# Attention and mixture of experts on one core: pairs of heads whole instead of by halves, and the place of some loads

## The chip, the core and the metric

The kernel runs on one core of one Trainium2 chip. The metric is the device time of one execution in microseconds (us). The profile is one further execution of the same program, taken by the hardware profiler.

## The reference

One layer on x of shape (4, 1024, 256), in float32. First attention with 16 heads of width 16, whose queries and keys are turned by position, and a layer norm over the residual sum:

```
q, k, v = x @ wq.T, x @ wk.T, x @ wv.T           # 16 heads of 16
q_embed = softplus(q) * (cos, sin)(position)     # width 32
k_embed = softplus(k) * (cos, sin)(position + bias of the head)
attn = softmax(q_embed @ k_embed.T / 4)          # 1024 x 1024 for each head and batch
x = layernorm(x + (attn @ v) @ wo.T)
```

Then a mixture of 8 experts, of which each token takes two and which holds 640 rows at most, with a second layer norm:

```
gates = softmax(x @ router_w + router_b); the two best experts of a token; a place in each expert's list
h = gelu(rows of the expert @ w1 + b1); out = h @ w2 + b2
x = layernorm(x + sum over a token's experts of gate * out)
```

## The kernel before

The changed parts all lie in the attention. Two heads make a *pair*; a batch has 8 pairs (two groups f of four), so there are 32 pairs in all. All work on a pair is cut into 8 *steps*, and the main loop runs over 256 steps, n = 0 to 255, with 64 to a batch. The order of instructions on every engine is the order in which this loop emits them.

For each pair the kernel needs two things. First the row maxima: `score_half` makes a 128 x 512 block of scores (a matmul, L755, into one of three PSUM banks of the pool `ps_3`) and VectorE takes the largest of each row (L759). A pair has 32 such blocks. From them `max_parts` makes the negated maxima in two parts (VectorE L771, ScalarE casts L772 and L773, VectorE L777), and `max_rows` turns them with four transposes (L783) and copies the result to `mt` (ScalarE, L785). Second, the pass itself: `key_scores` makes the scores again with the keys on the partitions (L795), `exponentials` adds the maxima with a two-row matmul (L809) and takes the exponential on ScalarE (L816), and `weighted_values` multiplies with the values (16 matmuls, L836) one step later.

A *unit* is what shares one set of maxima and one accumulator: a whole pair over 8 steps, or half of the queries of a pair over 4 steps. Before the change the first four pairs go by halves (eight units), all others whole. The maxima of a unit must be ready before it starts, so its score blocks are spread over earlier steps by a planner: the list `due` says that all blocks of unit w must be given out by two steps before its start, `may` says that a pair's blocks may not begin earlier than one step before the start of the pair before it, and each step takes the smallest number of blocks that keeps all due times. In a step TensorE runs: two score blocks, the key scores of the first tile, a third block, the key scores of the second tile, a fourth block, L809, the weighted values of the step before (L836), then any further blocks, then what the list `todo` has for this step (projections, embeddings of later pairs, values). If the step before used a PSUM bank for other work, the third block moves behind the second tile.

When a unit ends, `collect` sends the sums from its accumulator to two places with six transfers (L869, L872). When a group of four pairs ends, `over_sums` loads the collected denominators (`den`, L882), takes the reciprocal on VectorE (L884), stores it (`over`, L886) and loads it spread over the partitions with eight transfers (`r`, L889). For the second group of a batch this happens in the first steps of the next one: the load of `den` is emitted at the end of step 64b+1, the reciprocal, the store and the eight loads at the end of step 64b+2, and the products with `r` at the ends of steps 64b+5 and 64b+6.

`load_qk(i)` loads queries and keys of pair i, 2 MB in 12 transfers: six for the first head of the pair (its half 0), then six for the second head. The tiles have three buffers. Pair n/8 + 2 is loaded at the top of each step n that is a multiple of 8; the loop starts with pair 1's load already emitted, and pair 2 is loaded at step 4. All these transfers are issued by the one queue of SyncE (SP), strictly in the order of emission; an issue that waits holds up those behind it.

Ahead of the loop a prologue makes the tables, the embeddings of the first pairs and the maxima of the first unit. In its last part come, in this order: the second block of values (`vals[1]`), the second half of the query rows (`mq1`: for each of two heads four matmuls L460 and a copy L468), `max_parts(0)`, `max_rows(0)`, the stores of the second half of the query embeddings (`q1`), the tables' stores, and the copies `once` that free the buffer which pair 1's load then takes.

Of the kernel before, what the change touches and what calls it, by code (L numbers as in the profile page):

```python
# [28 lines left out]
def kernel(  # L29
# [20 lines left out]
    E, _, HID = w1.shape  # L50
    HD = 16
    NT = S // P
    NF = 2
    FH = 8
    NU = NF * FH // 2
# [46 lines left out]
    with ExitStack() as actx:  # L102
# [106 lines left out]
        def bias_angles():  # L209
            ps = bank("pbp", True)[:, 0:NF]  # L210
            for g in range(2):
                nc.tensor.matmul(
                    ps, place[:, g].rearrange("p d a j -> p (d a j)"), bias_in[:, g::2],
                    start=(g == 0), stop=(g == 1),
                )
            nc.vector.tensor_scalar(pb, ps, -2.0 * math.pi, 0.0, ALU.max, ALU.min)
            nc.scalar.activation(s1, pb, AF.Sin, scale=0.25)
            nc.scalar.activation(c1, pb, AF.Sin, bias=half_pi, scale=0.25)
            nc.scalar.preload_act_table_set("natural_log_exp_and_others")

            nc.vector.scalar_tensor_tensor(s2, s1, 2.0, c1, ALU.mult, ALU.mult)
            nc.vector.tensor_tensor(c2, s1, s1, ALU.mult)
            nc.vector.tensor_scalar(c2, c2, -2.0, 1.0, ALU.mult, ALU.add)
            nc.vector.scalar_tensor_tensor(sb4, s2, 8.0, c2, ALU.mult, ALU.mult)
            nc.vector.tensor_scalar(nb4, sb4, -1.0, None, ALU.mult)
            nc.vector.tensor_tensor(cb4, s2, s2, ALU.mult)
            nc.vector.tensor_scalar(cb4, cb4, -8.0, 4.0, ALU.mult, ALU.add)
# [502 lines left out]
        nms, mts, avs, pts = {}, {}, {}, {}  # L730


        units = []
        starts, lasting = [], []
        for i in range(B * NU):
            for h in range(2) if i < NU // NF else (None,):
                starts.append(starts[-1] + lasting[-1] if units else 0)
                units.append((i, *divmod(i // (NU // NF), NF), i % (NU // NF), h))
                lasting.append(NT if h is None else NT // 2)
# [21 lines left out]
        def max_parts(w):  # L761


            nm = nms.pop(w)
            m = m_sb[w % 2].rearrange("p i (s c) -> p i s c", c=32)
            both = small.tile([P, 4, 4, 2], F32, tag="nm_parts", name=f"nm_parts_{w}")
            least, of = both[:, :, :, 0], nm
            if units[w][4] is not None:
                least = least.rearrange("p i (t h) -> p i t h", t=2)
                of = nm[:, :, 0:2, :].unsqueeze(2).to_broadcast([P, 4, 2, 2, 2])  # L770
            nc.vector.tensor_reduce(least, of, AX.X, ALU.min)  # L771
            nc.scalar.copy(m.bitcast(F32R)[:, :, :, 0], both[:, :, :, 0])  # L772
            nc.scalar.activation(  # L773
                both.bitcast(F32R)[:, :, :, 1], both[:, :, :, 0], AF.Copy, scale=-1.0
            )
            yield
            nc.vector.tensor_reduce(m[:, :, :, 1], both, AX.X, ALU.add)  # L777
# [73 lines left out]
        def by_rows(w):  # L851
            return units[w][1] < B - 1 or units[w][2] == 0
# [75 lines left out]
        def run(pieces):  # L928
            next(pieces, None)
# [21 lines left out]
        for b in range(B):  # L951
# [17 lines left out]
            for n in range(4):  # L969
                w, h = "qk"[n // 2], n % 2  # L970
# [32 lines left out]
        with tc.manual_schedule():  # L1003
            bias_angles()
            once("k", 0)
            for i in range(2):
                transpose_x(0, i, rotate=True)
            nc.scalar.dma_start(wv_sb, wv)
            for w in "kq":
                load_twice(w, 1, nc.scalar)  # L1010
            for _ in key_table(0):
                pass
            once("q", 0)

            made = {}

            def first(w, h):
                return embedding(
                    0, 0, w, h, fast=(w, h) != ("q", 1), tab=cs if w == "q" else kt0,
                    pauses=(KC - 1,), rotate=True, apart=h == 1, made=made,  # L1020
                )

            def moving(w, h):
                return move_first(w, halves[h], made[w, h])

            k0, q0, k1, q1 = first("k", 0), first("q", 0), first("k", 1), first("q", 1)
            for work in (k0, k0):
                run(work)
            for i in range(2, 4):
                transpose_x(0, i, rotate=True)  # L1030
            table = key_table(1)
            for work in (q0, table, table, q0, k0, table, k1, q0, table, k1):
                run(work)
            mk0, mq0 = moving("k", 0), moving("q", 0)
            for work in (mk0, mq0, mk0, mq0, q1):
                run(work)

            for i in range(2):
                score_half(0, 2 * i, 0, True)
            for work in (k1, q1, q1):  # L1040
                run(work)
            for i in range(2, 4):
                score_half(0, 2 * i, 0, True)
            for work in (mk0, mq0, mk0, mq0, k0, q0):
                run(work)
            mk1 = moving("k", 1)
            run(mk1)
            for i in range(4):
                score_half(0, 2 * i + 1, 0, True)
            for work in (mk1, mk1, mk1, k1):  # L1050
                run(work)
            vals = [values_in_two(0, 0, h, rotate=True) for h in range(2)]
            for h in range(2):
                for i in range(4):
                    score_half(0, 2 * i + h, 1, True)
                    if (h, i) in ((0, 3), (1, 1)):
                        run(vals[0])
            for _ in vals[1]:
                pass
            mq1 = moving("q", 1)  # L1060
            for _ in range(4):
                run(mq1)
            for _ in max_parts(0):
                pass
            max_rows(0, rotate=True)
            run(q1)
            for h in range(2):
                store_table(0, h, cs[:, :, halves[h]])
                store_table(1, h, kt0[:, :, halves[h]])
            once("k", 1)  # L1070
            once("q", 1)
            load_qk(1)
            late_constants()
# [10 lines left out]
        with tc.manual_schedule():  # L1084
            for n in range(NS):
                w, c = step_of[n]
                b, p, t = n // (NU * NT), n // NT % NU, n % NT
                if n % NT == 0 and n > 0 or n == NT // 2:
                    i = n // NT + 2
                    if i < B * NU:  # L1090
                        load_qk(i)
                    elif i - B * NU < 2:
                        experts[i - B * NU] = expert_weights(i - B * NU)


                third_last, others[0] = others[0], False
                items = [(score_half, *x) for x in ahead[n]]
                first, third, fourth, rest = items[:2], items[2:3], items[3:4], items[4:]
                if third_last:
                    third, fourth = [], third + fourth  # L1100
                for f, *args in first:
                    f(*args)
                if parts:
                    run(parts)
                    parts = None
                tiles = [key_scores(w, c, 0)]
                for f, *args in third:
                    f(*args)
                tiles.append(key_scores(w, c, 1))
                for f, *args in fourth:  # L1110
                    f(*args)
                exponentials(w, c, tiles)
                if n > 0:
                    weighted_values(*step_of[n - 1])
                for f, *args in rest:
                    f(*args)
                if n + 2 in starts:
                    parts = max_parts(starts.index(n + 2))
                    run(parts)
                if n + 1 in starts:  # L1120
                    max_rows(starts.index(n + 1))
                if c == 1 and w > 0 and not by_rows(w - 1):
                    normalize(w - 1)
                for f, args in todo.get(n, ()):
                    f(*args)
                if b > 0 and (p, t) in FINISH:
                    if b not in finishing:
                        finishing[b] = finish_batch(b - 1)
                    next(finishing[b], None)
            weighted_values(*step_of[NS - 1])  # L1130


        with tc.manual_schedule():
            b, n = B - 1, NT // 2
# [328 lines left out]
```

## Time and profile before

| what | us |
|---|---|
| median of 3 runs (1423.34 to 1423.67) | 1423.62 |
| the profiled execution, its own time | 1425.13 |
| its span from the first to the last instruction | 1423.3 |
| TensorE busy | 1365.4 |
| VectorE busy | 885.8 |
| ScalarE busy | 740.8 |
| granted TensorE clock, mean over the span | 0.983 |

Times in the profile count from the first instruction of the span. PE is TensorE (PEld its weight loads), DVE VectorE, ACT ScalarE, POOL GpSimd, SP SyncE; a small q behind the name is an engine's sequencer, which issues transfers. A row of the timeline gives start, duration, engine, line, operation, result<-operands, shape and count; in square brackets the idle time before it and what ended that. A matmul's end is modelled, and matmuls overlap, so the length of a step is best read from the start of one L809 row to the start of the next.

### The profile page before, as it was taken

To read this page: it belongs to the slowest core of one execution; us is meant where nothing else is said; L and a number is where in the kernel's file an instruction comes from. 1 tells how busy PE (TensorE), PEld (TensorE's weight loads), DVE (VectorE), ACT (ScalarE), POOL (GpSimd) and SP (SyncE) were. 2 spreads that over 40 slices of the span, in tenths; PEclk is the share of its full clock that TensorE was granted. 3 is DMA by queue.
4 is the path that set the end of the run, shared out by engine and by line. 5 is a ranking of instruction groups with operands and counts; after the bars stand their busy time and mean duration, and the time that the engine had idled before them with its cause. 6 is when DMAs were issued, how large, how long until landed. Compare 5 with 4: busy or idle time off the path is not lost. (4 is left out here: it accounts for less than half of the span.)

```text
span 1423.3 us, 24542 instructions
## 1 busy us (share of the span) xinstructions
PE 1365.4 (96%) x9362; PEld 863.9 (61%) x9362; DVE 885.8 (62%) x1931; ACT 740.8 (52%) x1025; POOL 408.3 (29%) x427
## 2 busy tenths in 40 slices
PE   7999999999999999999999999999996399999998
PEld 4655555655655565565556556655643277777776
DVE  7667666667876666777856577887734433333335
ACT  5665676565566656556575665656463122222221
POOL 5261043340002646100065530000310314444443
PEclk9999999999999999999999999999998599999999
DMA  6776476374543746454466462225210436334211
GB/s 192 214 206 194 141 200 189 86 228 113 138 123 96 229 143 182 112 165 97 139 184 193 106 186 70 64 74 128 75 66 1 141 114 207 111 117 135 84 44 56
DMA packets 107765, 190.20 MB, mean 134 GB/s; under 512 B 19553, under 2 KB 56642, under 8 KB 107520
## 3 DMA queue, kind: packets, MB, share of 16 engines
q1 hardware_dynamic: 97792, 169.90, 41.2%
q0 software_dynamic: 8736, 16.87, 3.9%
q10 hardware_dynamic: 1120, 1.87, 0.4%
q8 instruction: 74, 1.21, 0.4%
q14 instruction: 43, 0.35, 0.1%
HBM read 118.27 MB, written 73.63 MB: 135 GB/s over the span
## 5 line engine op out<-in xcount | busy, mean ns | idle before, releaser
L759 DVE TENSOR_REDUCE nm<-s 128x1 f32<-128x512 f32 x1024 | 646.9, 683 | 234.1 <-PE s L755 226.0
L816 ACT ACTIVATE pt<-st 128x1024 f32<-128x1024 f32 x512 | 496.1, 1021 | 364.1 <-PE st L809 363.6
L755 PE MATMUL s<-qk 128*128 128x512 f32 x1024 | 383.4, 434 | 3.6 <-DVE nm L759 2.2
L795 PE MATMUL st<-qk 128*128 128x512 f32 x1024 | 303.8, 398 | 2.6 <-ACT pt L816 2.6
L836 PE MATMUL av<-pt,va 128*32 128x256 f32 x4096 | 274.7, 385 | 0.5 <-ACT pt L816 0.5
L755 PEld LDWEIGHTS s<-qk 128*128 128x128 f32 x1024 | 177.9, 188 | 110.5 <-DVE nm L759 49.4
L795 PEld LDWEIGHTS st<-qk 128*128 128x128 f32 x1024 | 182.7, 188 | 63.5 <-ACT pt L816 29.2
L836 PEld LDWEIGHTS av<-pt,va 128*32 128x32 f32 x4096 | 107.1, 109 | 107.0 <-issue 61.6
L692 POOL DMA_INDIRECT slots_in<-held,scatter_idx x64 | 63.0, 984 | 290.9 <-DVE scatter_idx L688 213.6
L414 POOL TENSOR_TENSOR soft_q<-y_q,soft_q 128x512 f32<-128x512 f32 x15 | 19.3, 1285 | 439.7 <-ACT soft_q L410 439.7
L1364 PE MATMUL op<-w,h 128*128 128x256 f32 x640 | 144.1, 379 | 0.0
L1345 PE MATMUL hp<-slots_t,w 128*128 128x320 f32 x512 | 141.0, 437 | 0.0
L1364 PEld LDWEIGHTS op<-w,h 128*128 128x128 f32 x640 | 119.5, 190 | 15.9
L809 PE MATMUL st<-mt,ones_r 2*128 2x512 f32 x1024 | 128.8, 492 | 0.0
L1345 PEld LDWEIGHTS hp<-slots_t,w 128*128 128x128 f32 x512 | 98.4, 192 | 40.4 <-issue 1.0
L809 PEld LDWEIGHTS st<-mt,ones_r 2*128 2x128 f32 x1024 | 49.0, 182 | 88.5 <-issue 88.1
L1352 ACT ACTIVATE h<-hp,b_sb 128x640 f32<-128x640 f32 x64 | 50.8, 793 | 87.7 <-PE hp L1345 87.7
L1379 DVE TENSOR_TENSOR o<-op,b_sb 128x256 f32<-128x256 f32 x35 | 14.9, 424 | 94.7 <-PE op L1364 94.6
L1380 ACT ACTIVATE o<-o,w 128x256 f32<-128x256 f32 x35 | 17.8, 508 | 103.2 <-issue 72.3
L1382 POOL DMA_INDIRECT y_rank<-o,rows x35 | 35.9, 1024 | 101.2 <-ACT slots_t L1195 46.1
L1303 POOL DMA_INDIRECT out_dram<-row,rows x40 | 40.9, 1022 | 42.7 <-DMA out_dram<-row,rows 13.1
L420 POOL TENSOR_TENSOR e_k<-soft_k,tab_k 128x512 f32<-128x512 f32 x28 | 35.4, 1286 | 47.5 <-DMA tab_k<-table 47.1
(217 smaller groups left out, 1034.5 us busy)
## 6 DMA issues: line engine op xcount, KB each, us to landing
qk<-embed_q SPq DMA_DIRECT2D x248, 128.0 KB
qk<-embed_k SPq DMA_DIRECT2D x124, 256.0 KB
embed_k<-parts_k SPq DMA_DIRECT2D x64, 256.0 KB
embed_q<-parts_q SPq DMA_DIRECT2D x64, 256.0 KB
w<-in_w_dram SPq DMA_DIRECT2D x16, 1024.0 KB
y_rank<-zero SPq DMA_DIRECT2D x8, 1024.0 KB
tab_q<-table SPq DMA_DIRECT2D x14, 512.0 KB
tab_k<-table SPq DMA_DIRECT2D x14, 512.0 KB
```

What stands on the lines that cost most here:

```text
L692: nc.gpsimd.indirect_dma_start(out=scatter_views[2 * t + k], out_offset=bass.IndirectOffsetOnAxis(ap=scatter_idx[:, k, t : t + 1], axis=0) ...
L755: nc.tensor.matmul(ps, qk[:, 2 * h, lo : lo + P], qk[:, 2 * h + 1, j * HS : (j + 1) * HS], start=True, stop=True,)
L759: nc.vector.tensor_reduce(nms[w][:, i, s, j : j + 1], ps, AX.X, ALU.max, negate=True)
L795: nc.tensor.matmul(ps[:, x, :], qk[:, 2 * h + 1, k * P : (k + 1) * P], qk[:, 2 * h, q * HS : (q + 1) * HS], start=True, stop=False,)
L809: nc.tensor.matmul(tiles[t][:, x, :], ones_r[rows, :], mts[w][rows, :], start=False, stop=True,)
L816: nc.scalar.activation(pt, tiles[t], AF.Exp)
L836: nc.tensor.matmul(av[32 * s : 32 * (s + 1), to], va[f][:, k, 2 * p + h, :], e, start=(c == 0 and n == 0), stop=(last and n == 1),)
L1303: nc.gpsimd.indirect_dma_start(out=out_views[t], out_offset=bass.IndirectOffsetOnAxis(ap=to[:, 0, t : t + 1], axis=0), in_=row[:, t, :], i ...
L1345: nc.tensor.matmul(ps[:, i, 0:half], w1_sb[:, k, c * P : (c + 1) * P], s_t[:, k, i * half : (i + 1) * half], start=(k == 0), stop=(k == KC ...
L1352: nc.scalar.activation(h_t[:, c, :].rearrange("p (i n) -> p i n", i=2), ps[:, :, 0:half], AF.Gelu, bias=b1_sb[:, e, c : c + 1],)
L1364: nc.tensor.matmul(ps, h_t[:, c, t * P : (t + 1) * P], w2_sb[:, c, :], start=(c == 0), stop=(c == HC - 1),)
L1382: nc.gpsimd.indirect_dma_start(out=y_views[e * ST + t], out_offset=bass.IndirectOffsetOnAxis(ap=to[:, 1, t : t + 1], axis=0), in_=o_sb, in ...
```

## The change

Three things are changed. Only pair 0 goes by halves of its queries; pairs 1, 2 and 3 become whole units. In the prologue `max_parts(0)` moves ahead of the second block of values, and `max_rows(0)` moves between the first and the second matmul group of `mq1`, so that on ScalarE the two casts of the maxima come before the copies of values and query rows. In the loop the loads of steps 64, 128 and 192 (pairs 10, 18 and 26) move to the top of steps 67, 131 and 195, behind the transfers of `over_sums`.

```diff
+        BY_HALF = (0,)
         units = []
         starts, lasting = [], []
         for i in range(B * NU):
-            for h in range(2) if i < NU // NF else (None,):
+            for h in range(2) if i in BY_HALF else (None,):
...
+            for _ in max_parts(0):
+                pass
             for _ in vals[1]:
                 pass
             mq1 = moving("q", 1)
-            for _ in range(4):
-                run(mq1)
-            for _ in max_parts(0):
-                pass
+            run(mq1)
             max_rows(0, rotate=True)
-            run(q1)
+            for work in (mq1, mq1, mq1, q1):
+                run(work)
...
-                if n % NT == 0 and n > 0 or n == NT // 2:
+
+                if t == 0 and p > 0 or t == 3 and p == 0 and b > 0 or n == NT // 2:
                     i = n // NT + 2
                     if i < B * NU:
                         load_qk(i)
```

Here NT is 8, NU is 8, b is the batch, p the pair within the batch and t the step within the pair.

## The prediction

> **What bounds the kernel now.** I read the page first, then the list of waits, then the timeline round the moved loads and in the first steps, and last the transfers by windows.
>
> ```profile
> span 1423.3 us, 24542 instructions
> PE 1365.4 (96%) x9362; PEld 863.9 (61%) x9362; DVE 885.8 (62%) x1931; ACT 740.8 (52%) x1025; POOL 408.3 (29%) x427
> ...
> PEclk9999999999999999999999999999998599999999
> ...
> L759 DVE TENSOR_REDUCE nm<-s 128x1 f32<-128x512 f32 x1024 | 646.9, 683 | 234.1 <-PE s L755 226.0
> ...
> L755 PE MATMUL s<-qk 128*128 128x512 f32 x1024 | 383.4, 434 | 3.6 <-DVE nm L759 2.2
> ```
>
> TensorE is busy in nearly every slice of the loop, VectorE waits for it (226 us) and hardly the other way round. So in the loop only two things cost time: work on TensorE, and waits of TensorE. The length of a step, from L809 row to L809 row, shows both:
>
> ```profile
> 67.65 0.50 PE L809 MATMUL st<-mt,ones_r 2*128 2x512 f32 x4
> ...
> 71.49 0.50 PE L809 MATMUL st<-mt,ones_r 2*128 2x512 f32 x4
> ...
> 331.53 0.50 PE L809 MATMUL st<-mt,ones_r 2*128 2x512 f32 x4
> ...
> 335.01 0.50 PE L809 MATMUL st<-mt,ones_r 2*128 2x512 f32 x4
> ```
>
> Step 5 with five score blocks takes 3.84, step 68 with four takes 3.48. Two steps stand out later, 66 with 4.46 and 130 with 4.68, and the timeline and the waits say why:
>
> ```profile
> 326.46 0.55 DVE L884 RECIPROCAL den<-den 128x64 f32<-128x64 f32 x1 [1.93 <-DMA den<-sums]
> ...
> 327.61 0.51 PE L755 MATMUL s<-qk 128*128 128x512 f32 x1 [0.69 <-DVE nm L759]
> ```
>
> ```profile
> DVE den L884 <- DMA den<-sums: 5.0, 3, 2.1
> ```
>
> VectorE stands before the reciprocal of the denominators, the score blocks behind it keep their banks, TensorE waits. What makes `den` late is on SP's queue (start, time to issue):
>
> ```profile
> 311.52 2.98 SPq L485 DMA_DIRECT2D qk<-embed_q  x4
> ...
> 321.88 0.49 SPq L872 DMA_DIRECT2D sums<-avs  x1
> 324.66 0.34 SPq L882 DMA_DIRECT2D den<-sums  x1
> 327.04 0.34 SPq L886 DMA_DIRECT2D over<-den  x1
> 328.51 4.33 SPq L889 DMA_DIRECT2D r<-over  x8
> ```
>
> Pair 10's load (12 issues, 311.52 to 318.8) stands ahead of the sums; the last sums need 2.7 us to land, against 1.6 us at step 192, where fewer bytes are ahead of them.
>
> **The change, part by part.** *Prologue.* Now ScalarE casts the maxima at 41.59, behind two query copies (40.20, 41.11), so L777 comes at 41.95, the transposes at 42.20, the loop's first score at 42.61. VectorE's L771 is done at 38.71. Moved up, casts (0.33) and L777 end at 39.3, under the values' matmuls (37.18 to 39.23). The query matmuls start at 38.99 as now, first group 1.1; transposes 0.5, to 40.6; then on ScalarE `mt` 0.6 and the first query copy 0.6, to 41.85. The first score needs that copy: 41.9 instead of 42.61, **-0.7**. The second copy ends at 42.4, its scores come about 1.2 after the first. SP: `q1` stores and tables keep their order. Pair 1's load, at 42.76, is released by `once` behind L777 on VectorE; it can go from 40.9, when the tables are issued.
>
> *Whole units.* The planner's rule, worked out by hand: before 6 blocks in step 0, 5 in each of steps 1 to 18, then 4; after 7 in steps 0 to 5, 6 in step 6, then 4. The blocks are the same, 16 come earlier. Removed: three `max_rows` with `max_parts` (steps 11, 19, 27), and 18 issues of `collect` from SP, which wait for nothing here. Whole and half units have the same L795, L809, L816 and L836.
>
> A seven-block step: the prologue's four scores in a row take 1.12 (30.77, five banks), so a block is 0.27 when no bank lacks: 3.84 + 0.54 = 4.38. But five blocks now stand in a row (three after L836, two of the next step) on three banks, and VectorE gives one back every 0.64 (26.8 us for 42 between 44.64 and 81.43). Step 0 shows the start of it, four in a row, two of them held 0.41:
>
> ```profile
> 45.08 1.89 PE L755 MATMUL s<-qk 128*128 128x512 f32 x4
> ...
> 46.46 0.19 PEld L755 LDWEIGHTS s<-qk 128*128 128x128 f32 x1 [0.41 <-DVE nm L759]
> ```
>
> I take 0.5 for it: 4.9. Lower end 4.5 (seven reductions at 0.64), upper 5.2 (both held blocks at the full 0.41). In steps 2, 4 and 6 the other work (values 1.7, embedding 1.6) parts the row, but waits itself for the first block's bank, 0.4 in the first two. Differences: step 0 +0.6, 1 +1.05, 2 +0.9, 3 +0.65 (transposes part the row), 4 +0.95, 5 +1.05, 6 +0.3: **+5.5** (3 to 7.5). Gained later: one block less is 0.36 (steps 8, 10, 12 to 14, 16 to 18: 2.6 with 0.2 of step 8's wait), 0.65 where transposes share the step (7, 15: 1.3), step 9's 1.0 (4.52 with a bank wait of 0.55), step 11's 1.05, step 19's 0.4, steps 26 to 28 1.2 (step 27 has 4.87 with transposes and a wait, 3.88 without): **-7.6** (-6.5 to -8). Pair 2's load (63.77, behind a table store that waits for POOL) must now serve scores at about 79.5 instead of step 10's at 91; it lands by 76 now, I add 2 for the slower steps: no wait.
>
> *Loads behind the sums.* The issue of the sums then waits for `avs` alone (done 317.84), the last sums go at 320.9, land at 322.6, `den` (1.8) at 324.4. VectorE comes at 324.53: no wait. The gain is step 66's excess, 4.46-3.48 = 0.98, and step 130's, 1.19; step 194 has none (3.48): **-2.2**.
>
> What is late next is the load. It is behind `over`, which waits for the reciprocal: 324.53 + 0.58, store to landing 1.47, eight `r` issues 3.6 to 4.3: the first issue is at 330.2 to 330.9, 3.2 to 3.9 after step 67's L809 (327.07, the wait gone). By the rule `may`, pair 10's scores begin in step 71. Step 70's L809 comes at 337.5; the first score, 1.4 later, needs half 0; the third, at 2.2 later = 339.7, half 1, so all 12 transfers. That is 8.8 to 9.5 us after the first issue. How long does a load take? One that starts with idle transfers, pair 11's, first issue at 341.84:
>
> ```profile
> 342.00:344.00 2.00, 2.00 (x26) 1.18 (x26) 1.03 (x2) 1.43 (x2) 0.00 (x0) 1.00 0.57 172
> ...
> 350.00:352.00 2.00, 2.00 (x18) 1.14 (x20) 2.00 (x5) 0.16 (x1) 0.00 (x0) 1.00 0.98 240
> 352.00:353.30 1.30, 1.30 (x19) 0.75 (x12) 0.54 (x1) 1.30 (x2) 0.00 (x0) 1.00 0.26 57
> ```
>
> The last two columns are the share of the 16 transfer engines and GB/s: the engines are full at about 240 GB/s till 352. By the trace's semaphore events half 0 lands 7.0, half 1 11.3 us after the first issue; the other loads take 10.9 to 12.6 , a few of the first batch up to 16.6. So half 0 (needed 7.9 to 8.7 after the first issue) is just in time and half 1 late. The nearest row is the clean load, 11.4, plus 0.4 for the tail of `r`: 11.8 against 9.2, a wait of TensorE of about 2.5 us, in steps 70 to 71, 134 to 135, 198 to 199: **+7.5** (1.4 to 3.5 each, 4 to 10.5). Nothing hides it; behind the third score stand the second tile's key scores, then L809, the exponentials and the weighted values. Nor is it given back: TensorE has no slack.
>
> [...] The trace has 11.3 for the clean load, so I take the trace.
>
> Sum: -0.7 + 5.5 - 7.6 - 2.2 + 7.5 = +2.5 on the profiled 1425.13 (1.8 of it around the span), 1427.6. It lies 1.5 above the median; the same difference gives **1426.1** there.
>
> **The rivals.** *The loads come in time.* The two waits for `den` go and nothing comes in their place: -5.0, 1418.6, faster. For it: half 0 suffices for two scores, and the queue is otherwise idle. Against: no load of the 31 landed in under 10.9 us, the need is at 9.5 at most. 12 in 100, since it would take a faster load than any here; another 5 for waits under 1.4.
>
> *The late load stops TensorE for longer than its clock stays up.* [...] Here the idle gap of 0.93 at step 130 cost no clock (granted 1.00 from 580 to 600), while after the loop's end, with TensorE idle most of the time, it was 0.50. With loads of 12.6 and a late first issue (8.8 to the need) each wait is 3.8; [...] 6 in 100.
>
> *VectorE becomes the bound of the first seven steps.* 7 x 0.64 = 4.5 is already above 4.38; [...]giving 5.2 and more for each: the +5.5 becomes +9, the sum +6, 1429.6. 9 in 100.
>
> That the change does less than it says: only if pair 10's scores began later; the planner's rule gives step 71.
>
> **How the numbers follow.** The main case has 68 in 100, its own range 1422.8 to 1429.1. About 0.2%, 2.85 us, is what this kernel's measurement can tell from no change. From 1426.5 on, slower: waits of 2.6 or more each, or dearer first steps, 31 of the 68; 35 within; 2 below. With the rivals: slower 31+6+9 = 46, same 35+2 = 37, faster 12+3+2 = 17. The range 1418.3 to 1430.5 takes in most of the timely case, and leaves out the clock and the sum of all upper ends.
>
> **What would show it.** Right: no DVE wait on `den` at steps 66 and 130, steps there 3.5; a PE wait on a DMA into `qk` at the third score (L755's line moved by one) of steps 70/71, 134/135, 198/199, 1.4 to 3.5 each; step 70 near 6; steps 1 and 5 near 4.9, step 11 at 3.5; the loop's first score 0.7 earlier. Wrong: those three steps at 3.5 (then faster), or first steps over 5.2 (then slower than said).

## The result and the profile after

The changed kernel takes 1434.07 us (median of 9 runs, 1426.96 to 1437.44). The kernel before, run beside it on the same chip, takes 1425.92 (median of 9 runs, 1423.34 to 1426.65). The ratio is 1.0053, with a 95% interval of 1.0041 to 1.0065: slower by about 7.5 us. The forecast was 1426.1 with a range to 1430.5, so it was wrong. It counted from 1423.62, the median of the first three of these nine runs of the kernel before; 2.3 of the 8.0 us by which it missed are this base, the rest is the change.

The runs of the changed kernel lie far apart, and they lie in the order of their granted TensorE clock: 1426.96 us at 0.983, 1430.13 at 0.981, three of 1431.78 to 1434.07 at 0.980, three of 1435.96 to 1436.02 at 0.977, and 1437.44 at 0.975. The one with the clock of the profile before (0.983) is only 3.4 above the kernel before's 1423.6. This suggests that about half of the loss comes from the clock, and the rest from something that every run has. As an estimate, the step in the clock from 0.983 to 0.975, times the span, is about 11 us, the size of the whole spread of 10.5.

The page of the profile after, in the lines that answer to those shown of before (the lines of the loop's work are higher by one than before):

```profile
span 1432.3 us, 24461 instructions
PE 1368.7 (96%) x9350; PEld 865.0 (60%) x9350; DVE 885.9 (62%) x1925; ACT 738.4 (52%) x1013; POOL 409.0 (29%) x427
...
PEclk9999999999999999999999999999998599999999
...
L760 DVE TENSOR_REDUCE nm<-s 128x1 f32<-128x512 f32 x1024 | 646.3, 683 | 248.7 <-PE s L756 240.2
L756 PE MATMUL s<-qk 128*128 128x512 f32 x1024 | 381.9, 433 | 9.6 <-DMA qk<-embed_k 4.1
```

There are 12 matmuls fewer and yet 3.3 us more of busy TensorE. The score matmuls' idle time is 9.6 us instead of 3.6, and the releaser named is now a load into `qk`. In the row of the clock, whose slices are 35.8 us long, nothing can be seen of a lost clock. The timeline shows the waits (TensorE, the reciprocal of step 66 first):

```profile
324.02 0.54 DVE L885 RECIPROCAL den<-den 128x64 f32<-128x64 f32 x1
...
341.76 0.47 PE L756 MATMUL s<-qk 128*128 128x512 f32 x1 [1.98 <-DMA qk<-embed_k]
...
605.04 0.47 PE L756 MATMUL s<-qk 128*128 128x512 f32 x1 [2.50 <-issue]
...
869.56 0.77 PE L756 MATMUL s<-qk 128*128 128x512 f32 x1 [2.07 <-DMA qk<-embed_k]
```

VectorE no longer stands before the reciprocal. In its place TensorE stands three times before the third score block of the step, whose operand is half 1 of pairs 10, 18 and 26. SP's queue (timeline of SP) has the order that the change asks for, and the load starts at 329.77:

```profile
322.04 0.32 SPq L883 DMA_DIRECT2D den<-sums  x1
324.59 0.33 SPq L887 DMA_DIRECT2D over<-den  x1
326.07 3.60 SPq L890 DMA_DIRECT2D r<-over  x8
329.77 2.54 SPq L485 DMA_DIRECT2D qk<-embed_q  x4
```

By the semaphore events half 0 lands 7.65 us after that, half 1 11.85 (341.62). The other two loads take 12.24 and 11.62.

What follows a wait is seen when the stretches are cut at the points at which the granted clock changes. In this trace these lie a multiple of 3.41 us apart (the half clock begins at 606.71 and at 869.53, 77 times 3.41 apart). So they do in the profile before (at 22.00 and 1090.37, 313 times 3.41), and in the traces of two experiments below (344.40 and 610.64, 78 times, with the loads alone; 341.84 and 870.90, 155 times, with the change once more). A *window* is from here on the stretch of 3.41 between two such points. The columns are the stretch, its length, the busy time of PE, PEld, DVE, ACT and POOL, then the granted clock, the share of the transfer engines and GB/s:

```profile
337.06:340.47 3.41, 2.71 (x25) 1.28 (x24) 3.18 (x7) 2.15 (x4) 0.00 (x0) 1.00 0.95 217
340.47:343.88 3.41, 2.12 (x20) 1.28 (x24) 1.41 (x3) 0.42 (x1) 0.00 (x0) 1.00 0.08 18
343.88:347.29 3.41, 3.41 (x27) 2.41 (x16) 1.44 (x3) 2.00 (x3) 0.00 (x0) 1.00 0.86 242
...
603.30:606.71 3.41, 1.67 (x12) 1.00 (x16) 1.16 (x2) 0.00 (x0) 0.00 (x0) 1.00 0.07 16
606.71:610.12 3.41, 3.41 (x22) 2.04 (x18) 0.23 (x1) 2.52 (x3) 0.00 (x0) 0.50 0.79 220
...
866.12:869.53 3.41, 1.37 (x12) 0.68 (x5) 1.91 (x4) 1.49 (x4) 0.00 (x0) 1.00 0.39 91
869.53:872.94 3.41, 3.38 (x16) 1.85 (x20) 1.38 (x2) 0.23 (x1) 0.00 (x0) 0.50 0.21 58
872.94:876.36 3.42, 3.42 (x20) 2.16 (x13) 0.00 (x0) 2.30 (x3) 0.00 (x0) 0.50 0.90 250
```

The wait of pair 10 falls across an edge: 0.70 us of idle TensorE in one window (3.41 - 2.71), 1.29 in the next, and the clock stays at 1.00. The wait of pair 18 leaves 1.74 in one window, and the next window runs at 0.50. The wait of pair 26 leaves 2.04, and two windows run at 0.50. TensorE counts as busy for 3.38 to 3.42 us of each of the three windows at 0.50, which fits the 3.3 us of added busy time.

The balance of the two profiled executions, worked out from L809 (after: L810) row to row, so that the first scores of step 71, which run ahead of its own row, count in step 70:

| part | forecast | after - before |
|---|---|---|
| start of the loop | -0.7 | -1.0 |
| steps 0 to 6 | +5.5 | +8.1 |
| steps 7 to 31 | -7.6 | -7.6 |
| steps 66, 130 (`den`) | -2.2 | -2.2 |
| steps 70, 134, 198 (late half 1) | +7.5 | +8.1 (2.23, 2.72, 3.17) |
| steps 135, 199 (half clock) | 0 | +3.6 (1.49, 2.09) |
| the rest | 0 | 0 |
| span | +2.5 | +9.0 |

The row of the late half 1 still holds a part of the clock's. The half clock begins at 869.53, inside step 198 (the L810 rows at its two ends; the four matmuls take 0.50 at the first and 0.80 at the second):

```profile
864.86 0.50 PE L810 MATMUL st<-mt,ones_r 2*128 2x512 f32 x4
...
871.53 0.80 PE L810 MATMUL st<-mt,ones_r 2*128 2x512 f32 x4
```

Steps 70 and 134, all at full clock, grow by 0.22 to 0.25 more than TensorE's idle time in them (1.98 and 2.50). Step 198 is idle for 2.07 and grows by 3.17, so some 0.9 of it is the clock's. As an estimate, then, the late load cost 7.3 and the clock 4.4.

### The profile page after: what moved, and what is told of

It is laid out like the page before. It is cut to its first block, busy times and chain, and to the rows that moved or that the text cites. A ratio compares the mean times of both kernels' runs of the same rounds, so it can differ in the third digit from the quotient of the medians.

```text
span 1432.3 us, 24461 instructions
## 1 busy us (share of the span) xinstructions
PE 1368.7 (96%) x9350; PEld 865.0 (60%) x9350; DVE 885.9 (62%) x1925; ACT 738.4 (52%) x1013; POOL 409.0 (29%) x427
## 5 line engine op out<-in xcount | busy, mean ns | idle before, releaser
L837 PE MATMUL av<-pt,va 128*32 128x256 f32 x4096 | 276.3, 387 | 0.5 <-ACT pt L817 0.5
L837 PEld LDWEIGHTS av<-pt,va 128*32 128x32 f32 x4096 | 107.7, 109 | 107.6 <-issue 62.7
L810 PE MATMUL st<-mt,ones_r 2*128 2x512 f32 x1024 | 129.3, 494 | 0.0
L810 PEld LDWEIGHTS st<-mt,ones_r 2*128 2x128 f32 x1024 | 49.2, 182 | 89.2 <-issue 88.9
L514 DVE TENSOR_TENSOR held<-po,held 128x512 f32<-128x512 f32 x32 | 22.1, 690 | 46.3 <-PE po L506 46.3
```

The costliest lines, as they stand in the source:

```text
L810: nc.tensor.matmul(tiles[t][:, x, :], ones_r[rows, :], mts[w][rows, :], start=False, stop=True,)
L837: nc.tensor.matmul(av[32 * s : 32 * (s + 1), to], va[f][:, k, 2 * p + h, :], e, start=(c == 0 and n == 0), stop=(last and n == 1),)
```

## The experiments

The theory after the result: the moved loads cost about 8 us of waiting, and a lost clock on top that varies from run to run; the whole units cost and give back nearly the same; the prologue and the sums' earlier transfer gain 3. One rival says that the seven-block steps carry the loss, another that the spread has nothing to do with the waits. The times of one chip are compared only with the kernel before on the same chip: its median was 1427.55 on the chip of the first four kernels, 1435.29 on that of the next four, 1427.8 on that of the last four.

**The moved loads alone**, in the kernel before:

```diff
-                if n % NT == 0 and n > 0 or n == NT // 2:
+                if t == 0 and p > 0 or t == 3 and p == 0 and b > 0 or n == NT // 2:
```

> Only the loads of steps 64, 128 and 192 move, nothing else. Theory A (the late loads carry the loss, and the clock makes it larger and uneven): the waits for den go (-2.2), three waits of 2.2 to 3.2 for half 1 of the pairs 10, 18, 26 come (+8), and each wait may take a window of 3.4 us of full clock with it (0 to 2 each, 1.5 to 2 us apiece): +6 without a lost window, up to +14 with many; the runs spread over several us and their times follow the granted clock. Theory B (the loss comes from the dense first seven steps, and so does the spread): about +1 or less, no spread.

Measured: 1436.76 (1434.82 to 1440.33), ratio 1.0065 (1.0048 to 1.0081). Steps 66 and 130 lose their 0.98 and 1.20. Steps 70 and 71 together gain 5.75, 134 and 135 gain 5.57, 198 and 199 gain 4.07. The windows at pair 10, cut at the points where the clock changes:

```profile
340.99:344.40 3.41, 1.09 (x4) 0.67 (x4) 1.14 (x3) 0.00 (x0) 0.00 (x0) 1.00 0.25 56
344.40:347.81 3.41, 3.41 (x25) 1.70 (x25) 0.80 (x2) 1.94 (x2) 0.00 (x0) 0.50 0.64 171
347.81:351.22 3.41, 3.41 (x10) 2.76 (x9) 1.35 (x3) 0.58 (x1) 0.00 (x0) 0.50 1.00 244
```

Here the edge fell so that 2.32 of idle lay in one window, and two windows were lost; the same happened at 610.64, and one window was lost at 876.88. By its ratio this one edit, run on another chip, accounts for the whole loss of the change and a little more.

**The whole units alone**, in the kernel before:

```diff
-            for h in range(2) if i < NU // NF else (None,):
+            for h in range(2) if i in (0,) else (None,):
```

> Only pairs 1 to 3 become whole units. Theory A: first seven steps +7 to +8, steps 7 to 31 -7.6, so 0 to +1, with no more spread than before; the first wait for half 1 of pair 1 in step 2 is about as long as with all changes. Theory B (the first steps carry the loss and the spread): +5 or more, with spread.

Measured: 1426.63 (1423.21 to 1434.01), ratio 0.9995 (0.9982 to 1.0008). Steps 0 to 6 gain 7.10, steps 7 to 31 lose 7.60. The seven-block steps do cost more than forecast, but they are paid back; the rival that they carry the loss falls. The expected wait in step 2 did not come: that step grows by 1.29, as much as steps 1 and 5. Half 1 of pair 1 lands at 55.35 here, and the loop, with the old prologue, starts 1.5 later than in the changed kernel. One run of the 14 lies apart, at 1434.01 (clock 0.979); the others end at 1428.69.

**The prologue alone**: the changed kernel with halves for the first four pairs and the loads at their old place.

```diff
-            for h in range(2) if i in BY_HALF else (None,):
+            for h in range(2) if i < NU // NF else (None,):
...
-                if t == 0 and p > 0 or t == 3 and p == 0 and b > 0 or n == NT // 2:
+                if n % NT == 0 and n > 0 or n == NT // 2:
```

> Only the order in the prologue changes. Both theories: the first L809 comes 1.0 us earlier, every step as before: -1.0. A rival for this part: pair 1's load[...] lands no earlier and the gain is lost in step 3: 0.

Measured: 1426.75 (1424.94 to 1431.54), ratio 0.9996 (0.9986 to 1.0006). The loop's first L809 is 0.80 earlier, but in the time of the whole nothing can be told. Its profile shows why a gain of 0.8 drowns: in this execution the sums came later than in the profile before, and the wait for `den` itself cost a window (timeline, then windows):

```profile
326.38 0.55 DVE L884 RECIPROCAL den<-den 128x64 f32<-128x64 f32 x1 [2.70 <-DMA den<-sums]
...
327.54 0.50 PE L755 MATMUL s<-qk 128*128 128x512 f32 x1 [1.50 <-DVE nm L759]
```

```profile
325.84:329.25 3.41, 1.91 (x22) 0.79 (x21) 2.87 (x5) 0.68 (x1) 0.00 (x0) 1.00 0.08 18
329.25:332.66 3.41, 3.41 (x13) 2.49 (x8) 1.92 (x4) 1.26 (x2) 0.00 (x0) 0.50 0.27 82
```

So the old place of the loads has the same trap, and the step after this one takes 1.54 more. The waits at steps 66 and 130 can be worth more than the 2.2 that the profile before shows.

**The wait filled with work.** The changed kernel, with ten matmuls of key tiles ahead of the waiting score in steps 71, 135 and 199. Each of the two groups is computed five times over before the one that counts, so TensorE works where it stood.

```diff
-        def key_scores(w, c, t):
+        def key_scores(w, c, t, fill=0):
...
+                for _ in range(fill):
+                    nc.tensor.matmul(
+                        ps[:, x, :],
+                        qk[:, 2 * h + 1, k * P : (k + 1) * P],
+                        qk[:, 2 * h, q * HS : (q + 1) * HS],
+                        start=True,
+                        stop=True,
+                    )
...
-                tiles = [key_scores(w, c, 0)]
+                tiles = [key_scores(w, c, 0, 5 if t == NT - 1 and p == 0 and b > 0 else 0)]
```

> All changes, and in steps 71, 135 and 199 ten extra matmuls into the first key tile (repeats of its own, overwritten by the last) in front of the score that waits; the result of the computation is the same. About 2.4 us of extra TensorE work stands where TensorE idles 2.2 to 3.2 us. Theory A: the clock stays at 1.00 through these steps, steps 71, 135, 199 take 4.9 as before, the spread goes, and the time is 3 to 4 us below the profiled changed kernel, near +5 over the kernel before. Theory C (the clock drops for another reason, or the lost time there isn't the clock): the same +8 to +9 with the same spread, or +16 if the filling adds its 7 us.

Measured: 1430.8 (1429.68 to 1431.37), ratio 1.0022 (1.0013 to 1.0031). Steps 70, 134 and 198 are 6.14, 5.75 and 5.99 us long against 5.71, 6.22 and 6.67 in the changed kernel. The extra matmuls stand where the waits stood: half 1 lands at 341.47, 604.32 and 867.27, and the score that needs it starts 0.14 to 0.35 later, when they are done. No window of the loop runs at half clock, and steps 135 and 199 are back at 4.90 and 5.19. The windows at pair 18:

```profile
601.41:604.82 3.41, 3.41 (x15) 2.79 (x16) 1.64 (x4) 1.23 (x4) 0.00 (x0) 1.00 0.53 125
604.82:608.23 3.41, 3.41 (x32) 2.07 (x31) 1.38 (x2) 1.99 (x3) 0.00 (x0) 1.00 0.47 131
```

The 11 runs lie within 1.7 us, at clocks of 0.981 to 0.983, where the changed kernel's spread over 10.5 on its chip and the kernel before's 32 runs over 7.4 on this one. This is the experiment that shows the clock's part: the load is as late as before (11.8 to 12.3 us after its first issue), and only the idleness is gone. Its span is 4.6 above the profile before, near what the table gives without the clock's estimated 4.4.

**The load split**: half 0 of the moved loads stays at steps 64, 128 and 192, half 1 goes behind the sums.

```diff
-        def load_qk(i):
+        def load_qk(i, heads=range(2)):
...
-            for h in range(2):
+            for h in heads:
...
-                if t == 0 and p > 0 or t == 3 and p == 0 and b > 0 or n == NT // 2:
+                if n % NT == 0 and n > 0 or t == 3 and p == 0 and b > 0 or n == NT // 2:
...
-                        load_qk(i)
+                        load_qk(i, (0, 1) if p or not b else (0,) if t == 0 else (1,))
```

> All changes, but of the moved loads only the second head's half (six transfers, 1 MB) goes behind over_sums; the first head's half stays at the top of steps 64, 128 and 192. Theory A: 1 MB less in front of the sums, den lands about 2 us earlier than before and VectorE does not wait (steps 66 and 130 at 3.5); half 1 has its six transfers landed about 7 us after its first issue, before the 9.4 us in which it is needed: steps 70, 134, 198 at 3.5, no lost clock there. The sum is -1.0 + 0.5 - 2.2 = -2.7 against the profiled kernel before, with a small spread. Rival (half a load is still late, or the sums still are): one of the two waits stays, -1 to +3.

Measured: 1430.09 (1428.37 to 1436.44), ratio 0.9958 (0.9939 to 0.9978), on the slower chip. Steps 66 and 130 take 3.5 and 3.48, and steps 70, 134 and 198 take 3.50, 3.49 and 3.50: neither the sums nor the load are late. On this chip all four kernels show stalls at steps 110, 174 and 238 to 243, in which VectorE and ScalarE stand still together for some 4 us; no trace of another chip has them, and what causes them is open.

**The prologue and the split load**, with halves for the first four pairs as before the change; on top of the split:

```diff
-            for h in range(2) if i in BY_HALF else (None,):
+            for h in range(2) if i < NU // NF else (None,):
```

> As e5_split_load, but with the first four pairs by halves as before; so the prologue's order and the split loads alone. Theory A: -1.0 - 2.2 = -3.2; whole units are worth about +0.5 of loss, so this is 0.5 to 1 below e5_split_load. Rival (whole units pay by themselves, through the transfers and casts they save): 1 or more above e5_split_load.

Measured: 1431.76 (1427.2 to 1437.05), ratio 0.9976 (0.9963 to 0.9988). Steps 66, 70, 130, 134 and 198 all take 3.5. That it comes out no better than the kernel with whole units cannot be taken as a verdict on the units, since the stalls of this chip are larger than the difference; the last group settles it.

**Pair 1's load ahead of the tables' stores**, on top of the split:

```diff
-            for h in range(2):
-                store_table(0, h, cs[:, :, halves[h]])
-                store_table(1, h, kt0[:, :, halves[h]])
             once("k", 1)
...
             load_qk(1)
+            for h in range(2):
+                store_table(0, h, cs[:, :, halves[h]])
+                store_table(1, h, kt0[:, :, halves[h]])
```

> As e5_split_load, and pair 1's load is issued ahead of the 2 MB of table stores instead of behind them. Theory A on step 2 (its extra 1.0 to 1.3 over the other seven-block steps with other work is the wait for half 1 of pair 1): the wait goes, half 1 lands about 12 us after the first issue at 40, step 2 takes about 6.8 instead of 7.9, the first seven steps +6.9 instead of +8.1, in all about -3.8. Rival (the wait is the bank of the score blocks): step 2 as before, and the tables come later for the embeddings: 0 or a loss.

Measured: 1432.27 (1426.75 to 1435.55), ratio 0.9976 (0.9966 to 0.9986). Step 2 is 1.29 longer than before the change instead of 1.75 with the split alone (2.34 in the changed kernel). This isolates a wait that the forecast had overlooked. In the changed kernel (timeline of TensorE):

```profile
55.51 0.93 PE L756 MATMUL s<-qk 128*128 128x512 f32 x3 [1.01 <-DMA wo_sb<-in_wo_dram]
```

The releaser named is a weight's load that came last by the profile; by the semaphore events what lands then is half 1 of pair 1, at 55.13, 14.4 after its first issue, which stands behind the tables' stores. With the load ahead of them it lands at 50.91 and the wait is gone. In the time of the whole no gain over the split alone can be told, since the intervals overlap. The wait is not the same in each execution: in the other traces that have both whole units and the new prologue, step 2 grows by 1.56 to 2.06.

**The loads ahead of `over` and `r`**: one step earlier than in the change, so behind the load of `den` alone.

```diff
-                if t == 0 and p > 0 or t == 3 and p == 0 and b > 0 or n == NT // 2:
+                if t == 0 and p > 0 or t == 2 and p == 0 and b > 0 or n == NT // 2:
```

> All changes, with the moved loads one step earlier: at the top of steps 66, 130, 194, behind the load of den and in front of the store of over and the eight loads of r. Theory A: den is early, so the first issue comes at 322.8 plus the issue of den, about 6.5 us earlier than with the change; half 1 lands before step 71 needs it, no wait and no lost clock there. But over and r now stand behind 12 issues (6 us) and 2 MB: r lands 4 to 5 us later, and the products with r at the end of step 69 make VectorE wait 2 to 3 us, of which TensorE loses 1 to 2 each time. In all -2.7 + 3 to 6 = 0 to +3. Rival (any load behind the sums is late for step 71): waits on qk stay, +5 or more.

Measured: 1451.92 (1449.35 to 1458.9), ratio 1.0125 (1.0099 to 1.015). This was expected near nothing and is by far the slowest. The load is in time (half 1 lands at 333.13), but `r` is now behind 2 MB: VectorE stands before the product with `r`, TensorE behind it (timeline, then the list of waits):

```profile
339.06 0.69 DVE L896 TENSOR_TENSOR num<-num,r 128x512 f32<-128x512 f32 x1 [4.68 <-DMA r<-over]
...
340.41 0.69 PE L756 MATMUL s<-qk 128*128 128x512 f32 x1 [3.68 <-DVE nm L760]
```

```profile
DVE num L896 <- DMA r<-over: 15.3, 3, 5.5
```

Steps 69, 133 and 197 take 4.15, 4.62 and 5.07 more, and each wait costs two windows of clock in the step behind it (at 341.03 the four matmuls L810 take 0.80 instead of 0.50, and L837 behind them 1.93 instead of 1.07). Three small transfers depend on each other here (`den`, `over`, `r`): before the change `den` stood behind the large load and was late, by 1.93 for VectorE at step 66; here it is `r`, by 4.68.

**Fewer halves, with the split load.** The kernel with prologue and split, pairs 0, 1 and 2 by halves:

```diff
-            for h in range(2) if i in BY_HALF else (None,):
+            for h in range(2) if i in (0, 1, 2) else (None,):
```

> Pairs 0, 1 and 2 by halves, pair 3 whole; the prologue's order as changed; only half 1 of the moved loads behind over_sums. The planner's blocks for each step are the same as before the change (6, then 5 up to step 18, then 4), so no dense first steps; only the maxima of one unit go, in step 27. Theory A: prologue -1.0, step 27 -1.0, waits for den -2.2, no wait for qk, no lost clock there: -4.2 step by step, and less spread than the kernel before. Rival (the gains are given back by a later wait): -2 or less.

Measured: 1421.93 (1421.01 to 1423.49), ratio 0.9954 (0.994 to 0.9968). And pairs 0 and 1 by halves, `(0, 1)` in the same line:

> As e9_halves_012 with pairs 0 and 1 by halves: 6 blocks in steps 0 to 4, 5 up to step 14. Theory A: a six-block step costs about 0.7 over a five-block one (a seven-block one cost 1.3), so steps 0 to 6 lose 3, and steps 7 to 31 gain 4 to 5 (two units' maxima gone, steps 15 to 18 with a block less): about -1 to -2 for both stretches, in all -4 to -5. Rival (dense steps cost more than the later gain): above e9_halves_012.

Measured: 1420.52 (1420.13 to 1421.24), ratio 0.9944 (0.993 to 0.9957), faster than both kernels. The planner now gives six blocks in steps 0 to 4 and five up to step 14. Steps 0 to 6 cost 2.18 and steps 7 to 31 give 4.15, a balance of -2.0; it is -0.5 with the seven-block steps of the whole units alone, and -1.35 with three pairs by halves. The span is 5.0 below the profile before, as expected; the ratio shows more, since the kernel before runs slower on this chip (1427.8) than where it was profiled (1423.6). Steps 66 and 70 and their like all take 3.48 or 3.49. The SP queue and VectorE at step 66 show the loads' halves parted:

```profile
320.11 0.34 SPq L882 DMA_DIRECT2D den<-sums  x1
322.63 0.34 SPq L886 DMA_DIRECT2D over<-den  x1
324.14 4.92 SPq L889 DMA_DIRECT2D r<-over  x8
329.11 1.81 SPq L485 DMA_DIRECT2D qk<-embed_q  x4
```

```profile
322.06 0.54 DVE L884 RECIPROCAL den<-den 128x64 f32<-128x64 f32 x1
```

Half 1 starts at 329.11, as late as the whole load did in the changed kernel, but it is 1 MB instead of 2 and lands at 335.88.

**The loads on another queue**: as the kernel with three pairs by halves, but the loads of steps 64, 128 and 192 whole, at their old place, and issued by GpSimd's queue instead of SP's.

```diff
-        def load_qk(i):
+        def load_qk(i, by=nc.sync):
...
-                        load_qk(i)
+                        load_qk(i, nc.sync if p or not b else nc.gpsimd)
```

> As e9_halves_012, but the whole loads of steps 64, 128, 192 stay at the top of these steps and are issued from GpSimd's queue instead of SP's. Theory D (order within SP's queue is what made the sums late): SP issues the sums as soon as avs is copied, they land in about 2 us, den is in time, steps 66 and 130 at 3.5: as e9_halves_012. Theory E (the shared transfer engines made them late): the sums still land 2.4 us or more after their issue behind the 2 MB, VectorE waits for den as before the change: 2 above e9_halves_012.

Measured: 1423.56 (1422.32 to 1424.74), ratio 0.9965 (0.9953 to 0.9977): 1.6 above the split, with intervals that overlap. SP's queue is free of the load, yet the sums are late (timelines of POOL, SP and VectorE):

```profile
309.41 2.08 POOL L485 DMA_DIRECT2D qk<-embed_q  x4
```

```profile
318.52 0.49 SPq L872 DMA_DIRECT2D sums<-avs  x1
...
322.17 0.32 SPq L882 DMA_DIRECT2D den<-sums  x1
```

```profile
323.78 0.55 DVE L884 RECIPROCAL den<-den 128x64 f32<-128x64 f32 x1 [1.55 <-DMA den<-sums]
```

The last sums take 3.6 us to land with no load ahead of them in their queue, against 1.6 in the changed kernel (issued at 320.40, `den` behind them at 322.04), where no load is on its way. They land about when the load does: by the semaphore events its last part is there at 322.18, and the issue of `den`, which waits for the sums, comes at 322.17. Steps 66, 130 and 194 take 4.09, 4.27 and 4.24 instead of 3.5, which is 2.1 in all. So the order of SP's queue is not needed to make the sums late. That they come late through transfer engines shared with the load would fit this, but which part of the path holds the sums up is not shown.

**The change once more**, on the chip of the last group:

> The changed kernel beside the three others on the same chip. Theory A: waits for half 1 of pairs 10, 18, 26 of 2 to 3.2 each, lost windows where 1.5 us or more of a wait lie in one 3.4 us window; +6 to +14 over the kernel before step by step, 10 or more above e9_halves_012.

Measured: 1433.0 (1430.12 to 1438.94), ratio 1.0038 (1.0022 to 1.0055). The loss is that of the first comparison, but the lost windows are others: now pair 10's wait fell wholly into one, and pair 18's did not (half clock at 341.84, behind 2.34 us of idle TensorE in the window before, and at 870.90, behind 1.46). On this chip the best kernel is 12.5 us below the change.

## Why the prediction was wrong

*The step that failed is the term of the clock, which the main case put at nothing.* The main case expected waits of 2.5, and the rival in which a wait costs clock was given 6 in 100. That waits of 2.5 leave the clock alone was the author's estimate; the longest wait it named in the loop before was the gap of 0.93 at step 130, at a clock of 1.00. The measurement decides otherwise: windows with 1.74 and 2.04 us of idle out of 3.41 were followed by half clock, at an estimated +4.4 in the profiled execution. The runs, which differ by up to 10.5, follow the clock. That rival had the direction right, but it counted on waits of 3.8, and the waits were 2.0 to 2.5.

Counted from TensorE's rows and the clock's changes within the loop, in all 14 traces: from full clock, an idle time of 1.46 to 3.27 in one window was followed by half clock 16 times and once was not (1.82); idle of 0.69 to 1.40 never was, in 21 such windows. The length of a wait alone doesn't decide it: the 1.98 of pair 10, parted by an edge into 0.70 and 1.29, kept the clock, and the 2.07 of pair 26, with 2.04 in one window, did not. Outside the loop the same line doesn't hold: the changed kernel lost a window behind 1.16 us of idle in the prologue (at 23.03), and behind the loop the kernel before kept the clock after a window with 1.73 (at 1086.96). So idle time as these rows give it is not exactly what decides; what is, isn't shown.

The trace of before already spoke against this estimate. In its prologue one window was lost (windows view of before):

```profile
18.59:22.00 3.41, 1.44 (x4) 0.58 (x4) 3.26 (x6) 2.92 (x7) 0.00 (x0) 1.00 0.42 154
22.00:25.41 3.41, 3.41 (x7) 2.05 (x8) 3.38 (x6) 2.32 (x4) 0.00 (x0) 0.50 0.98 362
```

TensorE is idle there for 1.98 us of the window, in two gaps of 0.99 and 1.13, both far below 2.5. The prediction named the gap of 0.93 at step 130, which cost nothing, and not this one.

*The first seven steps were mis-sized: +5.5 forecast, +8.1 measured.* A seven-block step takes 5.13 instead of 4.9 (steps 1 and 5: 1.28 and 1.29 over before, forecast 1.05), near the upper end of 5.2 that assumed both held blocks at the full 0.41. Step 3, for which the transposes were to part the row, took 1.33 instead of 0.65. And step 2 held the overlooked load: the prediction moved pair 1's load to 40.9 and looked at pair 2's need, but not at that of pair 1, whose half 1 TensorE now wants at 54.50, and which stands behind the tables' stores. It was issued 2.0 earlier than before the change and landed at 55.13, no earlier than before (54.91). That is 1.0 in this execution, as much as the earlier start of the loop gains.

*The other terms held.* The gain at steps 7 to 31 was -7.6 as forecast, and near it part by part (its eight steps at 0.36 with 0.2 come to 3.1 and not to the 2.6 set down; they measured 2.8); the waits for `den` went (-2.2); the loop started 1.0 earlier instead of 0.7. The late load was the right mechanism in the right place: first issue at 329.77 (forecast 330.2 to 330.9), 11.85 us to land (forecast 11.8), waits of 1.98, 2.50 and 2.07 (forecast 2.5 each). The rival by which the loads come in time is refuted by the same rows.

*The rival of VectorE* gave +9 for the first steps, close to the measured 8.1. But the kernel with whole units alone has 7.1 there, without the load's wait, and in step 1 of the changed kernel neither engine is the bound throughout (timeline of VectorE, then of TensorE's weight loads):

```profile
49.84 4.27 DVE L760 TENSOR_REDUCE nm<-s 128x1 f32<-128x512 f32 x7 [0.84 <-PE s L756]
```

```profile
49.30 0.53 PEld L756 LDWEIGHTS s<-qk 128*128 128x128 f32 x3 [0.41 <-DVE nm L760]
...
50.58 0.19 PEld L756 LDWEIGHTS s<-qk 128*128 128x128 f32 x1 [0.75 <-DVE nm L760]
51.18 0.19 PEld L756 LDWEIGHTS s<-qk 128*128 128x128 f32 x1 [0.41 <-DVE nm L760]
```

Seven reductions take 4.27, so 0.61 each, where 5.2 for seven would be 0.74, and ahead of them VectorE stands 0.84 without a block. TensorE's weight loads in turn stand 0.41, 0.75 and 0.41 for a bank in the row of five blocks. With three banks the two engines hold each other up within a step; that is the main case's mechanism, nearly at its upper end.

## What to carry to other kernels

When a large load is moved behind small transfers, compute when its last byte is needed and not when its first is; if only a part is needed late, move that part. A wait of TensorE is to be costed twice, once for itself (here 2.0 to 2.5 us) and once for the clock in the window after it (1.49 in step 135), and where the trace has several gaps, the line between those that cost clock and those that don't is to be read from them, the prologue's included. In this case run times that followed the granted clock (1426.96 at 0.983 to 1437.44 at 0.975) went with waits on both sides of that line, and filling the waits with work that changes nothing showed how much of the time it was (a spread of 1.7 instead of 10.5).

## What the hardware showed that was not expected

- Within the loop, idle TensorE of 1.46 us or more in one 3.41 us window was followed by one or two windows at a clock of 0.50 (16 cases; one window with 1.82 was not). One lost window lengthened the steps by 1.49 us (step 135 of the changed kernel) and by 1.54 (behind step 66 with the prologue alone); two cost about 3 with the loads alone, an estimate: steps 70 and 71 grow by 5.75 there, of which 2.49 is the wait and some 0.25 what grows beside it in the changed kernel. Whether one or two follow isn't told by the length of the wait: with the loads alone, waits of 2.49, 2.4 and 2.4 were followed by two, two and one.
- The changed kernel's nine runs spread by 10.5 us, in the order of their clock; with its waits filled, eleven runs on another chip spread by 1.7.
- A small transfer took 3.6 us to land while a 2 MB load issued from another queue was on its way, and 1.6 without it.
